# Where the later head pairs' position casts stand in an attention layer: other rounds, and the subtraction behind a round's last addition

## The chip, the cores and the metric

One core of a Trainium2 chip. The core has five engines, each with an instruction queue of its own: TensorE (PE, matrix products), VectorE (DVE), ScalarE (ACT), GpSimd (POOL) and SyncE (SP, which here only issues transfers). The metric is the device time of one execution of the whole program, in microseconds (us).

## The reference, cut to what matters

Eight images of 32 x 32 positions and 384 channels pass through a block with two layers. The part that the change touches is the attention of the first layer: six heads of width 64, with decomposed relative positions.

```python
# layer 0, x after a group norm; hw = 1024 positions, NH = 6, HD = 64
q, k, v = qkv[0], qkv[1], qkv[2]                      # (8 * 6, 1024, 64)
attn = jnp.einsum('bqd,bkd->bqk', q * SCALE, k)
rel_h = jnp.einsum('bhwc,hkc->bhwk', r_q, Rh)         # r_q is q as (b * NH, 32, 32, HD)
rel_w = jnp.einsum('bhwc,wkc->bhwk', r_q, Rw)
attn = attn.reshape(b * NH, h, w, h, w) + rel_h[:, :, :, :, None] + rel_w[:, :, :, None, :]
attn = jax.nn.softmax(attn.reshape(b * NH, hw, hw), axis=-1)
out = jnp.einsum('bqk,bkd->bqd', attn, v)
x = x + (out @ proj_w + proj_b)
```

Then follow a causal attention over the 1024 positions with one head of width 384, and, for five of the images, a feed-forward network (FFN) whose weights are binarized about group means and whose outputs are scaled by their largest absolute value.

## The kernel before, in words

**Images.** They are computed one after the other in the order 5, 0, 1, 2, 3, 4, 6, 7. Each runs through `layer0`, a projection, `attention1`, and, for images 0 to 4, the FFN.

**Pairs.** The six heads of layer 0 are handled as three pairs p = 0, 1, 2; the two heads of a pair lie on partitions 0 to 63 and 64 to 127. The text calls them pair 0, pair 1 and pair 2; pair 2 is the third.

**Position terms.** `positions(p)` (line 475) multiplies the queries with the tables of relative positions, and has the result written to memory and read back in another order (`near`). `place(p, near, pages)` (line 507) splits it in two parts[...]: for each of two halves d of the partitions ScalarE casts the values to the rounded type, `hi` (line 514, a 64 x 1024 copy), and VectorE subtracts, which leaves the remainder `lo` (line 515). Both lie in pages named `far`. Sixteen transfers then spread them over four pages `r`: the eight of `hi` are issued by SP, the eight of `lo` by GpSimd (line 522). For pair 0 this is done ahead of the attention. For pairs 1 and 2 `place` is a generator with two stops, called `later`, of which `attend0_fast` takes a piece of two steps (one pair) at a time.

**Rounds.** `attend0_fast` runs over (pair p, query half) in six rounds: (0, 0), (0, 1), (1, 0), (1, 1), (2, 0), (2, 1). The text calls them the first to the sixth. A round has these parts:

- `scores` (line 585), once for each of eight key tiles c of 128 positions: for the two heads two matmuls of queries and keys (line 590) into two tiles of PSUM, and two that add the position terms from `r` (line 594); then two exponentials on ScalarE (line 600) into a page `pr` of 128 x 1024.
- `add_up` (line 603): seven additions on VectorE (605 and 607) sum the eight pages to `sum0`, for the softmax's denominators. It returns the total and the sixth product's addition, `adds[4]`, the fifth of the seven.
- `reciprocals` (line 629) of the round before: two small matmuls into a PSUM tile `den` (line 633), behind this round's scores on PE; on VectorE, queued behind `adds[4]`, a reciprocal (637), `check` (two reductions to `seen`, lines 427 and 428; the one of line 427 reads `den` and is the tile's last reader), a broadcast copy to `wide` (641) and a transpose (642). GpSimd multiplies the output `oT` of the round before by it (line 659).
- `values` (line 610): 32 matmuls (line 615) of the exponentials with the values; ScalarE copies the result to `oT` (line 662).
- `over_tiles` (line 621): a transpose and a reduction on VectorE (624, 626), which make the operand `few` of the next `den`.

In the third round the image's input is loaded (`load_x`, SP) and GpSimd adds a bias to its eight pieces (`residual`, line 566, additions at 569), for use after the attention.

**PSUM.** All these matmuls write into tiles of one pool with eight banks, taken in turn; a tile's first write waits for the last reader of the tile that had the bank before. The score tiles of the fourth key tile come to the bank of the `den` tile of the round before.

**Order.** The lines are traced in this order, and a planner then fixes each engine's queue ahead of time by when it reckons an instruction's operands ready. `tc.issue_after(ins)` overrules it: what the block holds on `ins`'s engine is queued behind `ins` there. It sets an order of issue, not a wait for `ins` to finish, and does nothing to instructions on other engines. PE's order is written out by hand so (`behind_last`).[...]

For pair 1's pieces in the first round and pair 2's in the second, the kernel before asks this for ScalarE alone:

```python
if p == 0:
    with tc.issue_after(last_exp[0]):     # the round's last exponential, on ScalarE
        for _ in range(2):
            next(later, None)
```

So the casts stand behind all exponentials of the round, while the place of the subtractions on VectorE is left to the planner.

**Image 5**, the first, has work of its own in the same rounds: in its first, PE multiplies two weight matrices for the second layer (`multiply_out`); in its fifth (in the order of tracing) `binarize` is begun, which sums the FFN's weights group by group. The weights come by GpSimd in three loads (line 232), each a wide buffer, and each sum is a reduction on VectorE (line 250). The planner puts these where it reckons the loads landed, which may be rounds earlier than traced. Later pieces of `binarize` are taken between the key tiles of `attention1`.

A second, slower program for inputs outside the range stands behind a test at the end; it isn't executed with these inputs.

Of the kernel before, what the change touches and what calls it, by code (L numbers as in the profile page):

```python
# [11 lines left out]
F32 = mybir.dt.float32  # L12
# [3 lines left out]
ALU = mybir.AluOpType  # L16
# [9 lines left out]
NPAIR = NH // 2  # L26
# [49 lines left out]
def conv_attn_hybrid(  # L76
# [19 lines left out]
    nc = tc.nc  # L96
# [208 lines left out]
    def stages(pools):  # L305
# [120 lines left out]
        def check(total, reciprocal, i):  # L426
            nc.vector.tensor_reduce(seen[:, 0, i : i + 1], total, AX.X, ALU.add)  # L427
            nc.vector.tensor_reduce(seen[:, 1, i : i + 1], reciprocal, AX.X, ALU.add)
# [14 lines left out]
        def layer0(b, xT):  # L443
# [60 lines left out]
                            )  # L504
                return near, [page.bitcast(F32R) for page in pages]

            def place(p, near, pages):


                for d in range(2):  # L510
                    hi, lo, src = (t[ts(d, HD)].rearrange("k (h w) -> k h w", h=H) for t in (*pages, near))
                    if d:
                        src = near[ts(d, HD)].rearrange("k (w h) -> k h w", h=H)
                    nc.scalar.copy(hi, src)
                    nc.vector.tensor_tensor(lo, src, hi.bitcast(F32), ALU.subtract)  # L515
                    if d == 0:
                        yield
                for part in range(4):
                    for d in range(2):
                        for i in range(2):  # L520
                            half = part % 2 if d else part // 2
                            (nc.gpsimd if i else nc.sync).dma_start(  # L522
                                out=r[part][:, p, :].bitcast(F32).rearrange("(m i) t -> i m t", i=4)[2 * i + d],
                                in_=pages[i][ts(2 * d + 1 - half, 32)].bitcast(F32),
                            )
# [13 lines left out]
            near = []  # L539
# [9 lines left out]
            for j in range(NJ):  # L549
                values(j)  # L550
            r.extend(pools.image(f"r_{b}_{part}", F32R) for part in range(4))
            for _ in place(0, *near[0]):
                pass

            def others():
                for p in range(1, NPAIR):
                    yield from place(p, *near[p])
                    yield

            later = others()  # L560
            for _ in () if pools.fast else later:
                pass
            if pools.fast and b == ORDER[0]:
                join_biases(pools)

# [8 lines left out]
        def attend0_fast(residual, b, q, k, r, v, later):  # L574


            oT = pools.image(f"oT_{b}")

            rows = (slice(0, HD), slice(HD, P))
            last_exp, last_matmul = [None], [None]  # L580

            def behind_last():
                return tc.issue_after(last_matmul[0]) if last_matmul[0] is not None else contextlib.nullcontext()

            def scores(p, c, half):

                sc = [pools.o_tile(f"s0_{b}_{p}_{c}_{half}_{par}") for par in range(2)]
                with behind_last():
                    for par in range(2):
                        nc.tensor.matmul(  # L590
                            sc[par], k[rows[par], p, ts(c, P)], q[rows[par], p, ts(half, 512)], start=True, stop=False
                        )
                    for par in range(2):
                        last_matmul[0] = nc.tensor.matmul(  # L594
                            sc[par], unit[rows[par], c // 2 % 2].rearrange("i h w -> i (h w)"),
                            r[2 * (c // 4) + c % 2][rows[par], p, ts(half, 512)], start=False, stop=True,
                        ).ins
                pr = pools.page(f"pr0_{b}_{p}_{c}_{half}")
                for par in range(2):
                    last_exp[0] = nc.scalar.activation(pr[:, ts(par, 512)], sc[par], AF.Exp).ins  # L600
                return pr

            def add_up(p, half, prs):
                total = pools.page(f"sum0_{b}_{p}_{half}")
                adds = [nc.vector.tensor_tensor(total, prs[0], prs[1], ALU.add).ins]
                for pr in prs[2:]:
                    adds.append(nc.vector.tensor_tensor(total, total, pr, ALU.add).ins)  # L607
                return total, adds[4]

            def values(p, half, prs):  # L610
                av = pools.o_tile(f"av0_{b}_{p}_{half}")
                with behind_last():
                    for c, pr in enumerate(prs):
                        for par in range(2):
                            last_matmul[0] = nc.tensor.matmul(  # L615
                                av[ts(par, HD), :], v[:, c, ts(2 * p + par, HD)], pr[:, ts(par, 512)],
                                start=(c == 0), stop=(c == NJ - 1),
                            ).ins
                return av

            def over_tiles(p, half, total):

                tr = pools.page(f"tr0_{b}_{p}_{half}")
                nc.vector.transpose(tr, total)
                few = pools.small.tile([P, 2, 16], F32, tag="few", bufs=2, name=f"few_{b}_{p}_{half}")
                nc.vector.tensor_reduce(few, tr.rearrange("p (a n i) -> p a n i", a=2, i=32), AX.X, ALU.add)
                return few

            def reciprocals(p, half, few):
                den = pools.o_tile(f"den0_{b}_{p}_{half}")  # L630
                with behind_last():
                    for par in range(2):
                        last_matmul[0] = nc.tensor.matmul(
                            den[ts(par, HD), :16], fold.rearrange("p a i -> p (a i)"), few[:, par, :], start=True, stop=True
                        ).ins
                rt = pools.small.tile([P, 16], F32, tag="rt0", bufs=2, name=f"rt0_{b}_{p}_{half}")
                nc.vector.reciprocal(rt, den[:, :16])
                check(den[:, :16], rt, b * PER_IMAGE + 2 * p + half)
                room = pools.page(f"wide0_{b}_{p}_{half}")
                wide, rb = room[:, :512], room[:, 512:]  # L640
                nc.vector.tensor_copy(wide.rearrange("p (n i) -> p n i", i=32), rt.unsqueeze(2).to_broadcast([P, 16, 32]))
                nc.vector.transpose(rb, wide)
                return rb

            xt, waiting = None, None
            for p, half in itertools.product(range(NPAIR), range(2)):
                t, last = ts(half, 512), (p, half) == (NPAIR - 1, 1)
                prs = [scores(p, c, half) for c in range(NJ)]
                if b == ORDER[0] and (p, half) == (0, 0):
                    multiply_out(pools)  # L650
                if b == ORDER[0] and (p, half) == (2, 0):
                    signs.append(binarize(pools))
                    next(signs[0])
                total, late_add = add_up(p, half, prs)
                if waiting is not None:
                    p0, t0 = waiting[0], ts(waiting[1], 512)
                    with tc.issue_after(late_add):
                        rb = reciprocals(*waiting)
                    (nc.vector if last else nc.gpsimd).tensor_tensor(oT[:, p0, t0], oT[:, p0, t0], rb, ALU.mult)
                av = values(p, half, prs)  # L660
                if not last:
                    nc.scalar.copy(oT[:, p, t], av)
                if (p, half) == (1, 0):
                    xt = residual()
                if p == 0:
                    with tc.issue_after(last_exp[0]):
                        for _ in range(2):
                            next(later, None)
                waiting = (p, half, over_tiles(p, half, total))
            nc.vector.tensor_tensor(oT[:, p, t], av, reciprocals(*waiting), ALU.mult)  # L670
            with behind_last():
                begun = [project(wproj_sb, slice(0, C), oT, j, f"pj_{b}_{j}") for j in range(4)]

            def more(j):
                ps = begun[j] if j < 4 else project(wproj_sb, slice(0, C), oT, j, f"pj_{b}_{j}")
                nc.vector.tensor_tensor(xt[:, j, :], ps, xt[:, j, :], ALU.add)

            return xt, more
# [327 lines left out]
    with ExitStack() as scope:  # L1006
        pools = Pools(scope, tc, "f")
# [43 lines left out]
```

## Time and profile before

| | |
|---|---|
| Time, median of 3 runs | 2401.52 us (2399.17 to 2405.88) |
| The profiled execution | 2400.84 us |
| Its span, first to last instruction | 2399.1 us |
| Mean granted clock of TensorE | 0.992 |
| ScalarE busy | 1041.7 us (43%) |
| GpSimd busy | 329.9 us (14%) |
| Largest group of instructions on VectorE, the additions at line 607 | 377.4 us, 1311 ns each |
| Casts and subtractions for each image (lines 514 and 515) | six of each |

How to read it. The program is executed once with the hardware profiler on; all views come from this execution. The time is longer than the span by 1.7 us, which lie before the first and after the last instruction. Busy shares are means over stages with different limits. In the views an arrow `<-` inside a group's name stands for "made from", and an arrow after a duration names who released the waiting instruction; a number in square brackets at the end of a line is the idle time ahead of it. The two columns ahead of an instruction in a timeline are its start from the span's start and its duration, in us; `xN` says that N like it in a row are shown as one. In a table of stretches there follow the stretch's length and the busy time of PE, PE's weight loads, VectorE, ScalarE and GpSimd with the number of their instructions in brackets, the granted clock as a share of the full one, the mean busy share of the 16 transfer engines, and GB/s.

### The profile page before, as it was taken

Reading aid. Unit: us, or ns where it says so; the run is one execution under the profiler, and the core shown is the slowest. Engines: PE = TensorE matmul, PEld = TensorE weight load, DVE = VectorE, ACT = ScalarE, POOL = GpSimd, SP = SyncE. Lnnn points to the kernel's source line nnn. Section 1 sums busy time; section 2 is a strip of 40 time slices with the busy share of each in tenths; the row PEclk is TensorE's granted clock in tenths of the full one; section 3 lists DMA queues with packets and bytes.
Section 4 is the critical chain, followed back from the end, with each engine's and each line's share of the span. In section 5 each row is a group of like instructions: output and inputs, shape, how many; then the busy total and the mean of one; then the engine's idle time right before and its main releaser. Section 6 shows DMA issues by size and latency. Waiting matters only on the chain.

```text
span 2399.1 us, 26120 instructions
## 1 busy us (share of the span) xinstructions
PE 2347.1 (98%) x9442; PEld 1311.2 (55%) x9442; DVE 1441.9 (60%) x2302; ACT 1041.7 (43%) x1763; POOL 329.9 (14%) x421
## 2 busy tenths in 40 slices
PE   7899999999999999999999999999999999999998
PEld 3445544558644577445684455864457744554454
DVE  4585558655587347684455864558734668524851
ACT  3451155227463246551375522746424655115520
POOL 0310014000240001410002300024000131001300
PEclk9999999999999999999999999999999999999999
DMA  6610371220631012510108211053101271017100
GB/s 165 191 39 25 151 145 47 79 79 1 141 97 66 1 40 83 145 43 34 40 4 174 60 66 40 1 133 105 53 14 40 69 151 44 1 50 153 36 1 28
DMA packets 154795, 169.99 MB, mean 71 GB/s; under 512 B 113408, under 2 KB 126048, under 8 KB 153120
## 3 DMA queue, kind: packets, MB, share of 16 engines
q1 hardware_dynamic: 134416, 98.93, 16.4%
q0 software_dynamic: 17184, 69.22, 9.7%
q8 instruction: 77, 1.26, 0.2%
q10 hardware_dynamic: 3056, 0.08, 0.1%
q14 instruction: 62, 0.51, 0.1%
HBM read 75.38 MB, written 42.47 MB: 49 GB/s over the span
## 4 chain that ended last, share of the span: by engine, by line
PE 90%; DVE 5%; DMA 3%; SPq 1%; issue 1%; ACT 0%; POOL 0%; DVEq 0%; ACTq 0%
PE f_s L590 12%; PE f_av L615 11%; PE f_qk L438 10%; PE f_s L779 8%; PE f_av L792 8%; PE f_y L940 7%; PE f_y L899 7%; PE f_pj L386 5%; PE f_v L386 5%; PE f_q L738 5%; PE f_v L534 5%; PE f_s L594 4%; DVE f_sum L607 3%; PE f_rel L484 2%; DMA f_x<-in_x 1%; PE f_pt L314 1%
## 5 line engine op out<-in xcount | busy, mean ns | idle before, releaser
L600 ACT ACTIVATE f_pr<-f_s 128x512 f32<-128x512 f32 x768 | 413.5, 595 | 103.7 <-PE f_s L594 87.4
L590 PE MATMUL f_s<-f_q,f_k 64*128 64x512 f32 x1536 | 423.8, 611 | 27.3 <-DVE seen L427 27.3
L607 DVE TENSOR_TENSOR f_sum<-f_sum,f_pr 128x1024 f32<-128x1024 f32 x288 | 377.4, 1311 | 17.8 <-ACT f_pr L600 0.9
L615 PE MATMUL f_av<-f_pr,f_v 128*64 128x512 f32 x1536 | 339.3, 594 | 0.0
L594 PE MATMUL f_s<-f_r,unit 64*128 64x512 f32 x768 | 329.2, 808 | 0.2 <-DMA f_r<-f_far 0.2
L438 PE MATMUL f_qk<-f_gnT,wqkv_sb 128*128 128x512 f32 x576 | 257.3, 599 | 1.5 <-DVE f_gnT L349 1.5
L590 PEld LDWEIGHTS f_s<-f_q,f_k 64*128 64x128 f32 x1536 | 159.7, 191 | 157.5 <-issue 66.0
L615 PEld LDWEIGHTS f_av<-f_pr,f_v 128*64 128x64 f32 x1536 | 106.3, 137 | 196.4 <-issue 192.4
L779 PE MATMUL f_s<-f_q,f_lnT 128*128 128x512 f32 (+3 forms) x576 | 195.9, 488 | 0.0
L792 PE MATMUL f_av<-f_v,f_pr 128*128 128x385 f32 x576 | 195.3, 486 | 0.0
L438 PEld LDWEIGHTS f_qk<-f_gnT,wqkv_sb 128*128 128x128 f32 x576 | 108.0, 191 | 143.1 <-issue 131.1
L786 ACT ACTIVATE f_pr<-f_s 128x512 f32<-128x512 f32 (+3 forms) x96 | 47.1, 491 | 263.7 <-DVE f_s L784 217.6
L522 POOL DMA_DIRECT2D f_r<-f_far x192 | 102.6, 537 | 377.7 <-DVE f_far L515 343.9
L792 PEld LDWEIGHTS f_av<-f_v,f_pr 128*128 128x128 f32 x576 | 108.2, 190 | 77.3 <-issue 11.5
L779 PEld LDWEIGHTS f_s<-f_q,f_lnT 128*128 128x128 f32 x576 | 102.0, 190 | 77.8 <-issue 54.1
L594 PEld LDWEIGHTS f_s<-f_r,unit 64*128 64x128 f32 x768 | 86.6, 192 | 86.7 <-issue 83.1
L903 ACT ACTIVATE f_h<-f_y,b_sb 128x256 f32<-128x256 f32 x240 | 100.9, 471 | 67.3 <-PE f_y L899 67.3
L910 DVE TENSOR_REDUCE am<-f_h 128x1 f32<-128x1024 f32 (+2 forms) x80 | 71.6, 947 | 96.2 <-ACT f_h L903 96.2
L738 PE MATMUL f_q<-f_lnT,wqk 128*128 128x512 f32 x288 | 127.5, 592 | 0.0
L386 PE MATMUL f_pj<-wproj_sb,f_oT 128*128 128x384 f32 x384 | 127.3, 488 | 0.0
L386 PE MATMUL f_v<-wv_sb,f_lnT 128*128 128x384 f32 x384 | 126.5, 486 | 0.0
L534 PE MATMUL f_v<-wqkv_sb,f_gnT 128*128 128x384 f32 x384 | 125.1, 486 | 0.0
(153 smaller groups left out, 3036.0 us busy)
## 6 DMA issues: line engine op xcount, KB each, us to landing
f_far<-f_far SPq DMA_DIRECT2D x48, 512.0 KB, 3.2
f_r<-f_far POOLq DMA_DIRECT2D x192, 128.0 KB, 3.8
f_r<-f_far SPq DMA_DIRECT2D x192, 128.0 KB, 3.2
f_gnT<-in_xT SPq DMA_DIRECT2D x24, 512.0 KB, 4.6
f_x<-in_x SPq DMA_DIRECT2D x32, 384.0 KB, 6.4
out_y<-f_x POOLq DMA_DIRECT2D x28, 384.0 KB, 4.4
f_far<-f_far SPq DMA_DIRECT2D x128, 64.0 KB, 4.9
f_w1a<-w1s POOLq DMA_DIRECT2D x5, 1536.0 KB, 7.0
```

The source lines that it names most:

```text
L386: nc.tensor.matmul(ps[:, :C], xT[:, k, ts(j, P)], w[:, k, cols], start=(k == 0), stop=(k == NC - 1))
L438: nc.tensor.matmul(made[half], wqkv_sb[:, i, ts(m, P)], xT[:, i, ts(half, 512)], start=(i == 0), stop=(i == NC - 1))
L534: nc.tensor.matmul(ps, keys[:, i, j // 2, j % 2], wqkv_sb[:, i, 2 * C :], start=(i == 0), stop=(i == NC - 1))
L590: nc.tensor.matmul(sc[par], k[rows[par], p, ts(c, P)], q[rows[par], p, ts(half, 512)], start=True, stop=False)
L594: last_matmul[0] = nc.tensor.matmul(sc[par], unit[rows[par], c // 2 % 2].rearrange("i h w -> i (h w)"), r[2 * (c // 4) + c % 2][rows[par], ...
L600: last_exp[0] = nc.scalar.activation(pr[:, ts(par, 512)], sc[par], AF.Exp).ins
L607: adds.append(nc.vector.tensor_tensor(total, total, pr, ALU.add).ins)
L615: last_matmul[0] = nc.tensor.matmul(av[ts(par, HD), :], v[:, c, ts(2 * p + par, HD)], pr[:, ts(par, 512)], start=(c == 0), stop=(c == NJ - 1),
L738: nc.tensor.matmul(ps, wqk[:, k, ts(m, P)], xT[:, half, k, :], start=(k == 0), stop=(k == NC - 1))
L779: nc.tensor.matmul(sc[:, lo:], xT[:, c // 4, k, ts(c % 4, P)], q[:, half, k, lo:], start=(k == 0), stop=(k == NC - 1),)
L792: nc.tensor.matmul(av[:, : C + 1], prs[c][:, ts(j - c, P)], v[:, c, :], start=(c == 0), stop=(c == j))
L899: nc.tensor.matmul(ps, w1k[i // 2][:, ts(m, P)], xs[i % 2][:, half, i // 2, :], start=(i == 0), stop=(i == 2 * NC - 1))
```

## The change

`place` is an ordinary function now and takes two instructions, `behind`: the casts are queued behind the first of them on ScalarE, the subtractions behind the second on VectorE. `add_up` hands back all seven additions. `attend0_fast` calls for pair 1's casts in the first round, as before, and for pair 2's in the third instead of the second; in both the casts stand behind the round's last exponential, as before, and the subtractions behind the round's last addition. `reciprocals` stands behind the sixth product's addition, as before.

```diff
-            def place(p, near, pages):
-
+            def place(p, near, pages, behind=(None, None)):
+
+                def after(ins):
+                    return contextlib.nullcontext() if ins is None else tc.issue_after(ins)
 
                 for d in range(2):
...
-                    nc.scalar.copy(hi, src)
-                    nc.vector.tensor_tensor(lo, src, hi.bitcast(F32), ALU.subtract)
-                    if d == 0:
-                        yield
+                    with after(behind[0]):
+                        nc.scalar.copy(hi, src)
+                    with after(behind[1]):
+                        nc.vector.tensor_tensor(lo, src, hi.bitcast(F32), ALU.subtract)
...
-            for _ in place(0, *near[0]):
-                pass
-
-            def others():
-                for p in range(1, NPAIR):
-                    yield from place(p, *near[p])
-                    yield
-
-            later = others()
-            for _ in () if pools.fast else later:
-                pass
+            place(0, *near[0])
+
+            def later(p, *behind):
+                place(p, *near[p], behind)
+
+            for p in () if pools.fast else range(1, NPAIR):
+                later(p, None, None)
...
-                return total, adds[4]
+                return total, adds
...
-                total, late_add = add_up(p, half, prs)
+                total, adds = add_up(p, half, prs)
                 if waiting is not None:
                     p0, t0 = waiting[0], ts(waiting[1], 512)
-                    with tc.issue_after(late_add):
+                    with tc.issue_after(adds[4]):
                         rb = reciprocals(*waiting)
...
-                if p == 0:
-                    with tc.issue_after(last_exp[0]):
-                        for _ in range(2):
-                            next(later, None)
+                if half == 0 and p + 1 < NPAIR:
+                    later(p + 1, last_exp[0], adds[-1])
                 waiting = (p, half, over_tiles(p, half, total))
```

## The prediction

> **What bounds the kernel now.** I read four views, in this order: the page's busy times, the waits of PE, the timeline of one image around the longest of these waits, and a table of stretches over the same microseconds.
>
> The page, first and second block:
>
> ```profile
> span 2399.1 us, 26120 instructions
> PE 2347.1 (98%) x9442; PEld 1311.2 (55%) x9442; DVE 1441.9 (60%) x2302; ACT 1041.7 (43%) x1763; POOL 329.9 (14%) x421
> ```
>
> PE is busy for 98%, so only what PE does not do (52 us of idle), or does slowly, can be won. The waits of PE, in the view of waits limited to PE:
>
> ```profile
> PE f_s L590 <- DVE seen L427: 27.3, 8, 8.2
> PE f_gmean L336 <- DVE gmv L333: 10.8, 1, 10.8
> PE f_bad L201 <- DVE worst L199: 1.9, 1, 1.9
> ```
>
> More than half of the idle time is one wait, eight times: once per image. The score matmuls of the third round (pair 1, half 0) wait for `check`'s reduction `seen`, the last reader of a PSUM tile `f_den`, because the fourth key tile's scores take that tile's bank. Timeline of image 0 (image 5 is computed first, then 0, 1, 2, 3, 4, 6, 7), VectorE's instructions and then PE's:
>
> ```profile
> 356.98 1.22 DVE L605 TENSOR_TENSOR f_sum<-f_pr,f_pr 128x1024 f32<-128x1024 f32 x1
> 358.30 1.23 DVE L607 TENSOR_TENSOR f_sum<-f_sum,f_pr 128x1024 f32<-128x1024 f32 x1
> 361.19 1.22 DVE L515 TENSOR_TENSOR f_far<-f_far 64x1024 fp32r<-64x1024 f32 x1 [1.67 <-ACT f_far L514]
> 362.34 2.02 DVE L607 TENSOR_TENSOR f_sum<-f_sum,f_pr 128x1024 f32<-128x1024 f32 x1
> 364.39 2.56 DVE L515 TENSOR_TENSOR f_far<-f_far 64x1024 fp32r<-64x1024 f32 x1
> 366.98 3.82 DVE L607 TENSOR_TENSOR f_sum<-f_sum,f_pr 128x1024 f32<-128x1024 f32 x2
> 370.72 0.24 DVE L637 RECIPROCAL rt<-f_den 128x16 f32<-128x16 f32 x1
> 372.65 0.16 DVE L427 TENSOR_REDUCE seen<-f_den 128x1 f32<-128x16 f32 x1
> ...
> 369.36 1.02 PE L590 MATMUL f_s<-f_q,f_k 64*128 64x512 f32 x2
> 372.87 1.22 PE L590 MATMUL f_s<-f_q,f_k 64*128 64x512 f32 x1 [2.49 <-DVE seen L427]
> ```
>
> Pair 2's subtractions (L515) stand between the additions of the second round. They need ScalarE's casts (L514), which stand behind the round's last exponential, so VectorE idles 1.67 us with ready additions behind it; the reciprocal stands behind the sixth product's addition and comes 12 us after its matmul.
>
> The stretches (second round, third, fourth; the gap; what follows it):
>
> ```profile
> 349.93:365.99 16.06, 16.06 (x86) 6.84 (x85) 14.08 (x11) 12.29 (x19) 8.73 (x10) 1.00 0.81 226
> 365.99:388.63 22.64, 20.15 (x86) 10.68 (x85) 21.79 (x21) 9.25 (x17) 16.25 (x15) 0.85 0.28 75
> 388.63:404.69 16.06, 16.06 (x86) 6.90 (x84) 15.62 (x20) 9.23 (x17) 1.70 (x2) 1.00 0.00 0
> 370.38:372.87 2.49, 0.00 (x1) 0.00 (x0) 2.49 (x5) 0.33 (x1) 2.49 (x2) 0.85 0.00 0
> 372.87:378.20 5.33, 5.33 (x16) 4.20 (x18) 5.33 (x6) 2.09 (x4) 5.32 (x8) 0.50 0.20 44
> ```
>
> A round takes 16.06 us, the third 22.64. Of the 6.58 us over, 2.49 are idle; the rest is that PE then runs at half clock (0.50) for 5.33 us. From the timeline, the third round's excess over 16.06 is, in order of execution: 11.89, 6.58, 5.59, 3.66, 6.99, 5.34, 5.86, 3.87 us. Sum 49.8; without image 5, 37.9.
>
> **The Trainium skill.** "TensorE: Matmul & The Clock Gate", section "What's actually happening": an idle PE falls to half clock and needs about 3.4 us of work to come back. The trace agrees (0.50), though here a gap of 2.49 us is enough. "Perfetto Trace Analysis", section "Tensor Engine Instruction (MATMUL, LD_WEIGHTS)": VectorE's and ScalarE's queues are strictly first in, first out; the 1.67 us show it. "SBUF — State Buffer", section "Who interferes with whom": a VectorE instruction with two SBUF inputs and a GpSimd one that reads SBUF exclude each other. Agrees: beside GpSimd's L569 additions an addition takes 1.84 to 2.02 us, else 1.23, and L569 takes 1.94 us, else 0.97.
>
> **The change part by part.** It adds and removes no work: 32 casts, 32 subtractions and the same transfers. As built, PE's and SP's orders are unchanged; ScalarE's casts of pair 2 stand behind the third round's exponentials instead of the second's. VectorE's and GpSimd's orders move.
>
> *First round.* Additions no longer wait for the casts. In image 0 they start at 337.58 as now, one each 1.33 us, and the last ends at 346.8; casts end at 345.7 and 347.2; two subtractions 1.22 and 1.91, transpose 1.25, reduction 1.22 end at 352.2 (now 357.06). The den matmuls are at 358.86: covered by 6.7 us. Pair 1's GpSimd transfers leave with the subtractions, within 1 us of now (346.71, 349.79); they are needed at 366.
>
> *Second round.* No subtraction. Two exponential pairs are done at 353.5; five additions at 1.33 end at 360.1; reciprocal 0.25, an addition now beside L569 (1.9), `seen` 0.16: done at 362.5. PE needs it at 370.4. Cover 7.9 us, so the wait and the half clock behind it go. For the seven later images: **-37.9 us**. What is late next: nothing within the round, since PE then runs as in the fourth to sixth (9.06 us of scores, 7.0 of values).
>
> *Third round, which gets pair 2's work.* Starts 365.99. Exponentials allow additions from 369.6; L569 runs to 375.5, so three at 1.91 and two at 1.33: fifth done at 378.0. Reciprocal, addition, `seen` at 379.8, needed at 382.05+4.4=386.4: cover 6.6. Last addition 381, copy 0.42, then subtraction (casts done at 379.3), wide transpose 0.67, subtraction, transpose 1.25, reduction 1.22. The subtractions cost 1.22 to 2.6 each; I take 1.2 and 1.9 (the first pair in the trace): end 387.8, at worst 389.8. The den matmuls are at 391.0: cover 3.2, or 1.2. The fourth round's additions then start at 387.8 instead of 385.9; its `seen` comes at 395.9 and is needed at 402.5. By the fifth round VectorE is back in step.
>
> *Transfers of pair 2.* SP's eight follow the casts (376.1, 379.2) and are issued by 386. GpSimd's eight (0.53 each) stand behind the two `oT` multiplications (1.3 to 2.3) and end near 390, landing median 3.8: 394. The fifth round needs the first page at 398.7. Cover 5. SP's input loads stand ahead of them as now, and the next image's load stands behind them, at the sixth round. So the move itself costs nothing.
>
> *Image 5* has more on VectorE: the sums over the FFN weights (L250). As built, these now stand between the second round's additions, and GpSimd issues the first weight load behind all eight L569 additions instead of four. Eight at 0.97, two of them slowed, from 96 to 105; landing took 6.6 (99.98 to 106.61): 111.6. Three sums at 0.72 and three additions at 1.22 put the reciprocal at 117.4 and `seen` at 119.0, now 120.98: this stall shrinks by 2. Then the second weight load, into the same buffer, must wait for all five sums: issued near 125, its two parts landed at 130.6 and 133.2 (medians 5.1 and 7.0). Ten sums at 0.39 stand in front of the third round's additions: these start at 135.2, now 128.73. `seen` comes at 143.2 (6.45 to the reciprocal, 1.5 more), while PE, starting the fourth round at 134.4, needs it at 138.8. A new stall of 4.4, and half clock: in the seven images a mean wait of 2.7 costs 5.4, so 2.7 more. **+7.1 - 2.0 = +5.1 us**; bounds -2 (no new stall) and +12 (loads 5 us later).
>
> Sum: -37.9 + 5.1 = -32.8. The profiled execution took 2400.84 us (span 2399.1), the median of the runs is 2401.52. 2400.84 - 32.8 = 2368.0, or 2368.7 on the median's footing: **2369 us**.
>
> **Rivals.**
> 1. *Image 5 is freed too.* Loads land sooner than VectorE reaches them; -40 to -50: 2352 to 2361. For it: its wait is on a transfer, not on arithmetic. Against: two loads in one buffer, with sums in front of additions.
> 2. *The wait is partly handed on.* The third round's reduction comes after 391, so PE waits at den and runs cold in the fourth round. Cover is only 1.2 to 3.2 us. A miss of 0.5 us costs about that; with some half clock 2 per image, 16 in all: 2376 to 2390.
> 3. *Slower.* Pair 2's pages come too late for the fifth round: GpSimd's queue holds them behind `oT`, which waits for the wide transpose, and a subtraction waits for the cast. Against: 5 us of cover. It decides when they slip by 7.5 us: 2.5 of stall and 2.7 of half clock in eight images are 42 us against 32.8 won; 2410.
> 4. *It doesn't do what it says.* The bank is held by something else once the additions are early: 2400. Against: as built, PE's fourth key tile waits for just this `seen` in every round, and rounds four to six run without stall.
>
> **How the numbers follow.** Forecast (seven images freed, image 5 with one or two stalls, 2361 to 2375) 0.68; rival 1 0.10; rival 2 0.12; rival 3 0.06; rival 4 0.04. A measurement of this kernel tells some 0.3%, 7 us, from no change. Faster: 0.68 + 0.10 + most of rival 2 = 0.89; same 0.05; slower 0.06. The range takes the forecast with half of rivals 1 and 2: 2359 to 2381.
>
> **What would show it.** Right: in the seven images the third round takes 16.1 us, the wait of L590's scores for `seen` is left in image 5 alone, some 10 us in two pieces, and the clock is 1.00 in every other third round. The reduction of the third round ends before den's matmuls. Wrong: a wait of den for `few` or of the r matmuls for a transfer, a fourth round over 16.1 us in images after the first, or VectorE still idle in front of subtractions with additions behind.

## The result and the profile after

| | before | changed |
|---|---|---|
| Time, median | 2401.81 us (4 runs, 2399.17 to 2405.88) | 2371.46 us (4 runs, 2370.05 to 2372.34) |
| Ratio to before, 95% interval | | 0.9873 [0.9858, 0.9888] |
| The profiled execution, and its span | 2400.84 us, 2399.1 us | 2370.05 us, 2367.9 us |
| Excess of the third round over 16.06 us, seven images, sum | 37.9 us | 0.0 us |
| Image 5: excess of its third and fourth round | 11.9 and 0.0 us | 10.6 and 7.35 us |

The change is 1.3% faster. The page after, its first lines (span; busy time, share of the span and instructions of each engine):

```profile
span 2367.9 us, 26177 instructions
PE 2332.1 (98%) x9442; PEld 1291.8 (55%) x9442; DVE 1431.8 (60%) x2302; ACT 1042.0 (44%) x1763; POOL 312.2 (13%) x421
```

PE is still busy for 98%, of a span that is 31 us shorter. The view of PE's waits (total, times, longest):

```profile
PE f_s L588 <- DVE seen L427: 11.9, 2, 7.4
PE f_gmean L336 <- DVE gmv L333: 10.8, 1, 10.8
```

The wait for `seen` is left twice instead of eight times, and both are in image 5. (Lines behind the diff are two lower than before, so the scores are L588 and L592; inside it the subtractions are now L519 and the transfers of the pages L524.) The table of stretches for image 0, second, third and fourth round, answers to the one shown of before:

```profile
357.74:373.80 16.06, 16.06 (x86) 6.84 (x84) 14.44 (x15) 9.18 (x17) 8.64 (x11) 1.00 0.71 207
373.80:389.87 16.07, 16.07 (x87) 6.91 (x85) 13.43 (x15) 12.31 (x19) 6.51 (x8) 1.00 0.12 29
389.87:405.93 16.06, 16.06 (x87) 6.93 (x85) 15.53 (x18) 9.22 (x17) 6.99 (x9) 1.00 0.38 103
```

The third round took 22.64 us and takes 16.07; PE's clock is 1.00 in it. VectorE's timeline in the same image shows why:

```profile
362.72 5.21 DVE L605 TENSOR_TENSOR f_sum<-f_sum,f_pr 128x1024 f32<-128x1024 f32 x4
367.85 0.25 DVE L635 RECIPROCAL rt<-f_den 128x16 f32<-128x16 f32 x1
368.04 1.23 DVE L605 TENSOR_TENSOR f_sum<-f_sum,f_pr 128x1024 f32<-128x1024 f32 x1
369.18 0.17 DVE L427 TENSOR_REDUCE seen<-f_den 128x1 f32<-128x16 f32 x1
...
388.28 1.21 DVE L519 TENSOR_TENSOR f_far<-f_far 64x1024 fp32r<-64x1024 f32 x1
389.42 0.69 DVE L640 STREAM_TRANSPOSE f_wide<-f_wide 128x512 f32<-128x512 f32 x1
390.14 1.97 DVE L519 TENSOR_TENSOR f_far<-f_far 64x1024 fp32r<-64x1024 f32 x1
392.14 1.25 DVE L622 STREAM_TRANSPOSE f_tr<-f_sum 128x1024 f32<-128x1024 f32 x1
393.42 1.22 DVE L624 TENSOR_REDUCE few<-f_tr 128x32 f32<-128x1024 f32 x1
```

The read of `den` now ends at 369.35, 4.45 us before the third round begins (before: 6.82 us after its beginning). Pair 2's subtractions, at 388.28 and 390.14, cost 3.2 us of VectorE, and the reduction still ends at 394.64 with the `den` matmuls at 398.79.

The span is shorter by 31.2 us: 37.9 won in the seven images, 6.0 lost in image 5, and 0.7 lost elsewhere: 1.56 us before image 5's first round (it starts at 72.03 instead of 70.47, in work that the change doesn't touch), of which 0.9 come back in small pieces.

Image 5's two stalls, from VectorE's timeline of the changed kernel:

```profile
98.94 1.84 DVE L605 TENSOR_TENSOR f_sum<-f_sum,f_pr 128x1024 f32<-128x1024 f32 x1
114.71 0.79 DVE L250 TENSOR_REDUCE sums_w<-f_w 128x1 f32<-128x614 f32 x1 [13.92 <-DMA f_w<-in_w1T]
115.42 1.22 DVE L605 TENSOR_TENSOR f_sum<-f_sum,f_pr 128x1024 f32<-128x1024 f32 x1
...
121.55 0.17 DVE L427 TENSOR_REDUCE seen<-f_den 128x1 f32<-128x16 f32 x1
...
126.14 1.48 DVE L250 TENSOR_REDUCE sums_w<-f_w 128x1 f32<-128x614 f32 x2
132.62 4.09 DVE L250 TENSOR_REDUCE sums_w<-f_w 128x1 f32<-128x307 f32 x10 [5.00 <-DMA f_w<-in_w1T]
136.62 1.22 DVE L603 TENSOR_TENSOR f_sum<-f_pr,f_pr 128x1024 f32<-128x1024 f32 x1
```

Each time a weight sum that waits for its load (13.92 us, then 5.00) stands ahead of additions whose operands are ready.

### The profile page after: what moved, and what is told of

Same layout as the page of the kernel before. It is cut to its first block, busy times and chain, and to the rows that moved or that the text cites. A ratio compares the mean times of both kernels' runs of the same rounds, so it can differ in the third digit from the quotient of the medians.

```text
span 2367.9 us, 26177 instructions
## 1 busy us (share of the span) xinstructions
PE 2332.1 (98%) x9442; PEld 1291.8 (55%) x9442; DVE 1431.8 (60%) x2302; ACT 1042.0 (44%) x1763; POOL 312.2 (13%) x421
## 3 DMA queue, kind: packets, MB, share of 16 engines
q8 instruction: 77, 1.26, 0.2%
## 4 chain that ended last, share of the span: by engine, by line
PE 95%; DVE 2%; DMA 1%; POOL 0%; issue 0%; ACT 0%; SPq 0%; DVEq 0%; POOLq 0%; ACTq 0%
PE f_s L588 13%; PE f_av L613 13%; PE f_qk L438 11%; PE f_s L775 8%; PE f_av L788 8%; PE f_y L936 7%; PE f_y L895 7%; PE f_pj L386 5%; PE f_v L386 5%; PE f_v L536 5%; PE f_q L734 5%; PE f_s L592 3%; PE f_rel L484 2%; PE f_pt L314 1%; DVE f_sum L605 1%; PE f_den L631 0%
## 5 line engine op out<-in xcount | busy, mean ns | idle before, releaser
L588 PE MATMUL f_s<-f_q,f_k 64*128 64x512 f32 x1536 | 404.7, 600 | 11.9 <-DVE seen L427 11.9
L605 DVE TENSOR_TENSOR f_sum<-f_sum,f_pr 128x1024 f32<-128x1024 f32 x288 | 364.4, 1265 | 22.4 <-DVE rt L635 0.6
L592 PE MATMUL f_s<-f_r,unit 64*128 64x512 f32 x768 | 311.5, 797 | 0.0
L588 PEld LDWEIGHTS f_s<-f_q,f_k 64*128 64x128 f32 x1536 | 148.1, 188 | 140.7 <-issue 74.1
L524 POOL DMA_DIRECT2D f_r<-f_far x192 | 102.5, 536 | 462.3 <-DVE f_far L519 418.9
L592 PEld LDWEIGHTS f_s<-f_r,unit 64*128 64x128 f32 x768 | 76.9, 188 | 91.2 <-issue 90.7
```

The lines of the kernel that those rows point to most:

```text
L588: nc.tensor.matmul(sc[par], k[rows[par], p, ts(c, P)], q[rows[par], p, ts(half, 512)], start=True, stop=False)
L592: last_matmul[0] = nc.tensor.matmul(sc[par], unit[rows[par], c // 2 % 2].rearrange("i h w -> i (h w)"), r[2 * (c // 4) + c % 2][rows[par], ...
```

## The experiments

All times below are medians, beside runs of the kernel before on the same chip. "Seven" is the sum of the excess over 16.06 us in the second to fifth rounds of the seven images other than 5.

| kernel | median us | ratio to before, 95% | seven, us | image 5's excess, us |
|---|---|---|---|---|
| second_gated | 2365.56 | 0.9845 [0.9829, 0.9862] | 0.0 | 12.9 and 0.8 |
| third_free | 2362.10 | 0.9835 [0.9819, 0.9852] | 0.8 | 9.1 and 0.1 |
| first_free | 2362.15 | 0.9832 [0.9816, 0.9849] | 0.0 | 9.4 and 0.0 |
| sums_late | 2354.39 | 0.9797 [0.9781, 0.9813] | 0.0 | 0.0 |
| sums_spread | 2354.36 | 0.9801 [0.9787, 0.9815] | 0.0 | 0.0 |
| read_late_3 | 2377.58 | 0.9897 [0.9880, 0.9913] | 4.2 | 20.2 |
| read_late_5 | 2404.98 | 1.0012 [1.0004, 1.0021] | 30.1 | 23.1 |
| read_late_7 | 2434.46 | 1.0135 [1.0118, 1.0152] | 51.8 | 26.4 |
| before_read_early | 2425.48 | 1.0101 [1.0084, 1.0118] | 43.6 | 10.4 |
| fourth_round | 2419.01 | 1.0069 [1.0053, 1.0085] | 41.9 | 10.2, 7.6 and 7.3 |

First rounds aren't counted: image 5's carries other work, in every kernel alike, and one of another image is now and then 1 us longer for a transfer. The time of a kernel isn't the sum of its row: other stages differ by 1 to 2 us between kernels, and `before_read_early` loses 2.15 us more in each image's last round.

### Which part of the change brings it

Pair 2's casts back in the second round, with the order on VectorE kept:

```diff
-                if half == 0 and p + 1 < NPAIR:
-                    later(p + 1, last_exp[0], adds[-1])
+                if p == 0:
+                    later(half + 1, last_exp[0], adds[-1])
```

> The changed kernel, but pair 2's casts go back to the second round; its subtractions stand behind that round's last addition. Theory A (only the place of the subtractions on VectorE matters: the additions and the read of the den tile must not stand behind them): the third round of images 0 to 4, 6, 7 takes 16.06 us as with the change, the reduction of the second round ends near 31 us after the round before began and PE's den doesn't wait. Rival B (the second round has no room for this work, the move is what helps): the den matmuls of the third round wait for the reduction, or the third round takes 1 to 4 us over 16.06 in the seven images, 7 to 28 us in all. Image 5: the sum over the second weight load stands between the third round's fourth and fifth addition instead of ten sums before the first one, so its second stall (7.35 us over) falls to 0 to 2 and the first stays near 10.6. In all A: 2363 to 2367 us; B: 2371 to 2395.

Measured: 2365.56 us, no excess in the seven images; the second round's reduction ends 1.9 to 3.9 us before `den` needs it. Rival B falls: the second round has the room. The move isn't needed if the order is there. Image 5's first stall is 12.9 us, where I had expected it to stay near 10.6.

The move alone, subtractions left to the planner:

```diff
-                    later(p + 1, last_exp[0], adds[-1])
+                    later(p + 1, last_exp[0], None)
```

> The changed kernel without the order on VectorE: pair 2's casts in the third round, subtractions placed by the planner, which puts pair 2's behind the second and the third addition of the third round. Theory A, worked out from the changed kernel's trace of image 0: casts end at 385.5 and 387.0, so subtractions and additions run until the reciprocal at 392.5, the read of den ends at 394.0, and PE needs it at 394.3: the fourth round takes 16.1 to 17.5 us in the seven images, so that the move alone brings nearly everything, 2365 to 2385. Rival C (the order is what helps, the move only carries the stall one round on): the fourth round is 4 to 7 us over in each, as the third was before, 2395 to 2405. Image 5: its five first sums now stand ahead of the second round's additions and one of the second load's between them, first stall 13 to 18 us, second 0 to 3.

Measured: 2362.10 us, below the range that I gave; the fourth round takes 16.16 to 16.20 us in the seven images. Rival C falls too. VectorE's timeline of image 0 in this kernel (its third round began at 363.92):

```profile
371.76 2.12 DVE L605 TENSOR_TENSOR f_sum<-f_sum,f_pr 128x1024 f32<-128x1024 f32 x1
375.14 1.22 DVE L519 TENSOR_TENSOR f_far<-f_far 64x1024 fp32r<-64x1024 f32 x1 [1.26 <-ACT f_far L517]
376.28 1.21 DVE L605 TENSOR_TENSOR f_sum<-f_sum,f_pr 128x1024 f32<-128x1024 f32 x1
377.52 1.95 DVE L519 TENSOR_TENSOR f_far<-f_far 64x1024 fp32r<-64x1024 f32 x1
379.50 2.48 DVE L605 TENSOR_TENSOR f_sum<-f_sum,f_pr 128x1024 f32<-128x1024 f32 x2
381.91 0.25 DVE L635 RECIPROCAL rt<-f_den 128x16 f32<-128x16 f32 x1
382.07 1.17 DVE L605 TENSOR_TENSOR f_sum<-f_sum,f_pr 128x1024 f32<-128x1024 f32 x1
383.17 0.17 DVE L427 TENSOR_REDUCE seen<-f_den 128x1 f32<-128x16 f32 x1
```

The subtractions stand between additions, and VectorE idles 1.26 us for a cast, as in the kernel before. But GpSimd's bias additions, beside which VectorE's took longer in the kernel before, are over at 370.40, before the first of these lines, and the read ends 3.35 us into the fourth round, 0.1 late. So each half of the change frees the seven images by itself. The move alone does it with nothing to spare; the order alone (`second_gated`) has 6.3 to 7.7 us of cover for the read and 1.9 for the reduction.

The order taken off in the first round only:

```diff
-                    later(p + 1, last_exp[0], adds[-1])
+                    later(p + 1, last_exp[0], adds[-1] if p else None)
```

> The changed kernel, but pair 1's subtractions in the first round aren't held behind the last addition; pair 2's are, in the third. Theory A: in the seven images nothing changes (no round over 16.1 us), since the first round's reduction has 6.7 us of cover; that part of the change is worth nothing there. In image 5 the planner then puts five sums ahead of the second round's additions and one of the second load's between them: first stall 13 to 18 instead of 10.6, second 0 to 3 instead of 7.35; 2367 to 2376. Rival: the first round's part carries some of the gain, the second or the third round of the seven images is 2 to 6 us over again, 2385 to 2400.

Measured: 2362.15 us, below what I expected and 9.3 us faster than the change. In the seven images nothing moves, as expected. In image 5 the planner now puts GpSimd's first weight load between its bias additions again (issued at 101.12 us, not 107.34), which shortens the first stall and takes the second away; my 13 to 18 us for the first stall assumed the late load. So the first round's part of the change brings nothing and, through the planner, costs 8.5 us in image 5 (17.9 of excess against 9.4), more than the 6.0 that image 5 lost. The expectation for image 5 was wrong for `third_free` in the same way.

### Image 5

The weight sums behind the last multiplication of the attention (`sums_behind[0]`):

```diff
-            nc.vector.tensor_tensor(oT[:, p, t], av, reciprocals(*waiting), ALU.mult)
+            sums_behind[:] = [nc.vector.tensor_tensor(oT[:, p, t], av, reciprocals(*waiting), ALU.mult).ins]
...
-                    next(work, None)
+                    with tc.issue_after(sums_behind[0]):
+                        next(work, None)
...
```

> The changed kernel with the FFN weights' sums of image 5 held on VectorE behind the last multiplication of its attention. Theory A (the two stalls of image 5 are its weight sums standing ahead of additions): image 5's third and fourth round take 16.1 us like the others', 17.9 us won there; the sums (3.6 us and 4.1 us of VectorE) then stand among the projection's additions, which costs 0 to 4 us; 2352 to 2358. Rival (image 5's stalls come from elsewhere, from the transfers of pair 2 or the multiplication of the weight matrices): the third or the fourth round stays 4 us or more over; 2362 to 2372.

Measured: 2354.39 us, 17.1 us less than the change; all of image 5's rounds from the second on take 16.05 to 16.12 us. PE's waits of this kernel, the longest first:

```profile
PE f_gmean L336 <- DVE gmv L333: 11.4, 1, 11.4
PE f_bad L201 <- DVE worst L199: 1.9, 1, 1.9
PE f_qk L438 <- DVE f_gnT L349: 1.5, 1, 1.5
PE f_pt L314 <- DVE f_xn L376: 1.5, 2, 1.2
```

The wait for `seen` is gone. The price is in the last line: 1.5 us of waiting for the layer norm behind the attention, where the sums now stand. So I spread them, begun in the fourth round, two pieces behind each round's last addition and the rest as above:

```diff
-                if g % 2:
+                if g in (2, 4):
                     yield False
...
-                if b == ORDER[0] and (p, half) == (2, 0):
+                if b == ORDER[0] and (p, half) == (1, 1):
...
+                if b == ORDER[0] and signs:
+                    with tc.issue_after(adds[-1]):
+                        for _ in range(2):
+                            next(signs[0])
...
```

> The changed kernel with image 5's weight sums spread: binarize is begun in the fourth round, the first load's five sums stand behind the fourth round's last addition, the second load's ten behind the fifth's and the sixth's, the last five behind the last multiplication. Theory A: each place has room (VectorE reads den 6 to 7 us ahead of need in these rounds), so all six rounds of image 5 stay as in the other images, and the 1.5 us that the layer norm waited in the kernel with all sums at the end go too: 2352 to 2355 us, at most 1.5 below that kernel. Rival: a sum waits for its load in front of VectorE's other work, and the fifth or sixth round of image 5 is 1 us or more over: 2355 to 2365.

Measured: 2354.36 us, no different. The layer norm's wait fell to 0.3 us, and a wait of `den` for the reduction, 1.87 us, came behind the last round: five sums stand in front of that reduction. So not every place had the room that I had assumed.

### What PE waits for, and what lateness costs

In the second round, reciprocal and read stand behind the round's reduction and behind 3, 5 or 7 added reductions that compute nothing of use:

```diff
...
+                few, behind = None, adds[4]
+                if (p, half) == (0, 1):
+                    few = over_tiles(p, half, total)
+                    behind = last_few[0]
+                    for _ in range(5):
+                        with tc.issue_after(behind):
+                            behind = nc.vector.tensor_reduce(spare, wqkv_sb[:, 0, :T], AX.X, ALU.add).ins
...
-                    with tc.issue_after(adds[4]):
+                    with tc.issue_after(behind):
...
```

> The changed kernel, but in the second round the reciprocal and the read of den are queued on VectorE behind the round's transpose and reduction and behind three added reductions of 128x1024 (1.22 us each) over a weight tile, whose results nobody uses. Theory A (PE needs that read by 4.4 us into the third round and by nothing earlier): counted from image 0 of the changed kernel's trace, the last addition ends near 371, the reduction at 373.4, the read near 377.4, PE needs it at 378.2: the third round of the seven images stays at 16.1 us, although VectorE reads den 8 us later than with the change. Rival D (the cover isn't what I worked out, something else of the read's chain is needed earlier): the third or fourth round takes 1 us or more over 16.06. Image 5 may move by up to 8 us either way. A: 2363 to 2380 us in all, D: 2380 to 2400.

> The same with five added reductions. Theory A: the read ends near 379.9 where PE needs it at 378.2, a gap of some 1.7 us in each of the seven images. If such a gap costs its own length alone: third rounds of 17.8 us, 12 us in all; if PE falls to half clock behind it as behind the gaps of 2.5 to 3.1 us before the change, 1.1 to 4.1 us more in each: 18.9 to 21.9 us. Rival D's price (the read isn't what PE waits for): no change against three.

> The same with seven. Theory A: a gap of 4.1 us in each of the seven images, half clock behind it for sure, 1.1 to 4.1 us more: third rounds of 21.3 to 24.3 us, the stall of before the change and more, with the subtractions behind the additions all the same; 2405 to 2432 us. Rival D: no change against three.

With five and seven reductions the stall came back at its old place, with the subtractions behind the additions all the while. What was delayed is the whole of `reciprocals` on VectorE, not its read alone; but PE's view names only `seen` for these rounds, and the round's reduction, now ahead of it, ends 9.5 us or more before the matmuls of `den`. Rival D's forecast for five and seven, no change, failed. Its sign for three, a round 1 us or more over, did come: four images are 0.6 to 1.4 us over, two of them more than 1, because the read is needed at 3.2 us and not at the 4.4 that I had worked out. `read_late_7` lies 2.5 us above its range; much of what these three lose is in image 5 (20 to 26 us), where the delayed read stands behind weight sums as well. The three kernels, with those above, give a curve. "Read" is the end of the read (L427, here L428) after the start of the round that needs the bank, "excess" that round's time over 16.06 us:

| read, us | excess, us | where |
|---|---|---|
| 3.21 to 3.22 | 0.0 | read_late_3, three images |
| 3.33 to 3.37 | 0.10 to 0.14 | third_free, seven |
| 3.83, 4.19, 4.45, 4.61 | 0.60, 0.97, 1.23, 1.39 | read_late_3, the other four |
| 5.71 to 5.72 | 2.5 | read_late_5, two |
| 6.34 to 6.39 | 4.7 to 4.85 | read_late_5, four |
| 6.88 and 7.09 | 3.7 and 3.9 | before, two |
| 6.82 to 7.42 | 5.3 to 7.0 | before, the other five |
| 7.56 | 6.0 | read_late_5, one |
| 8.23 to 8.92 | 6.4 to 8.0 | read_late_7, seven |

Up to 2.5 us of lateness against 3.23 us the excess is that lateness, to 0.03 us. Beyond, half clock comes on top: in the seven images 0 to 3.0 us, near 1.67 in half of the cases (the last section has the reason). PE's clock (last column but two) behind the gap in image 0 of `read_late_5`:

```profile
384.30:387.00 2.70, 2.70 (x8) 1.51 (x10) 2.56 (x5) 0.17 (x1) 1.36 (x1) 0.50 0.00 0
387.00:390.00 3.00, 3.00 (x18) 1.39 (x14) 2.90 (x2) 2.29 (x5) 0.73 (x1) 0.92 0.02 5
```

The other way round: the kernel before, where only the read comes earlier, behind the fourth product's addition:

```diff
-                return total, adds[4]
+                return total, adds[2]
```

> The kernel before with one number changed: the reciprocal and the read of den stand behind the fourth product's addition instead of the sixth's, in every round; casts and subtractions stay in the first and second round, one of pair 2's subtractions still between the second round's additions. Theory A (the bank's release is all that PE waits for): in image 0's trace of before the first subtraction ends at 362.4, one addition, the read near 366, PE needs it at 370.4: the third round falls from 19.7 to 23 us to 16.1 in the seven images, 37.9 us won without moving a cast. Image 5 gets five weight sums ahead of the second round's additions and one of the second load's ahead of its reduction: its excess is 6 to 16 us against 11.9. In all 2358 to 2370. Rival E (the subtractions among the additions, or the time at which pair 2's pages are ready, hold PE in another way as well): third or fourth round 1 us or more over in the seven images, 2372 to 2400.

Measured: 2425.48 us, 23.8 slower than before; my expectation failed, and rival E's range of 2372 to 2400 was too low as well. Its longest wait of PE (total, times, longest):

```profile
PE f_den L633 <- DVE few L626: 48.3, 16, 4.5
```

And a piece of VectorE's timeline of image 0:

```profile
366.95 0.16 DVE L427 TENSOR_REDUCE seen<-f_den 128x1 f32<-128x16 f32 x1
...
374.04 2.57 DVE L515 TENSOR_TENSOR f_far<-f_far 64x1024 fp32r<-64x1024 f32 x1
376.64 1.25 DVE L624 STREAM_TRANSPOSE f_tr<-f_sum 128x1024 f32<-128x1024 f32 x1
377.92 1.22 DVE L626 TENSOR_REDUCE few<-f_tr 128x32 f32<-128x1024 f32 x1
```

The read ends at 367.11, 0.5 us into the third round that began at 366.61, and the wait for `seen` is gone in the seven images, so the bank was what PE waited for. But the round's reduction ends at 379.1, and `den` is due at 375.5: a second limit, as late as the first, had stood behind it. The kernel before has it too (its reductions end 3.1 to 3.8 us after the `den` matmuls would be due in an unstalled round), and no wait shows it there, because PE was already late. What stood between the additions made everything behind them late, read and reduction; in the changed kernel the second round's reductions end 6.7 to 8.1 us before `den` needs them.

### How late pair 2's pages may come

The casts one round later still, in the fourth:

```diff
-                if half == 0 and p + 1 < NPAIR:
+                if (p, half) in ((0, 0), (1, 1)):
                     later(p + 1, last_exp[0], adds[-1])
```

> The changed kernel, but pair 2's casts one round later still, in the fourth; order on VectorE as in the change. Tests the slower case of the prediction (pair 2's pages too late for the fifth round) and the 5 us of cover that the change leaves it. From image 0 of the changed kernel: the second GpSimd transfer, with which the first page is whole, is issued by 393.7 and lands 3.9 later, 397.6, the last near 400.8; the fifth round needs the first page at 406.5. A round later these are 413.6 and 416.9: PE's position matmuls of the fifth round wait 7 to 10 us for a transfer in each of the eight images, and half clock adds 0 to 3: fifth rounds of 23 to 29 us, 56 to 106 in all, 2427 to 2477 us. Rival (the pages aren't what bounds the place, VectorE is): the loss is in the reads of den or in the reductions, and the fifth round stays at 16.1.

Measured: 2419.01 us. The fifth round of the seven images takes 21.5 to 23.2 us, 49.2 us over in all with image 5's; I had expected 23 to 29 and at least 2427. In GpSimd's timeline of image 0 (fifth round from 412.93) the second transfer, the first of the last line, completes the first page:

```profile
411.51 0.72 POOL L524 DMA_DIRECT2D f_r<-f_far  x1 [12.75 <-DVE f_far L519]
412.26 2.62 POOL L657 TENSOR_TENSOR f_oT<-f_oT,f_wide 128x512 f32<-128x512 f32 x1
414.83 3.72 POOL L524 DMA_DIRECT2D f_r<-f_far  x7
```

It is issued at 414.8 to 415.4, and the first position matmul, due 0.57 us into the round, runs at 417.50. PE's view of waits names no releaser there (30.5 us stand under "issue"), so that PE waited for this transfer is worked out from the order of the transfers. If so, it landed within some 2.1 us, where I had taken the median of 3.9, and its issue came 1.4 us earlier in its round than in the changed kernel, where bias additions run beside VectorE's. The direction is shown: the fifth round's position matmuls are what is late (the reads that it needs end 4.7 us or more before it begins), so the pages bound how far the casts may move. One round is free and two are not.

## Why the prediction was right

2369 us were predicted, 2371.46 measured; for the profiled execution 2368.0 and 2370.05.

- **The seven images, -37.9 us: right** to the tenth; their third rounds take 16.05 to 16.08 us.
- **The cover of the read.** Predicted 7.9 us, from a read 3.5 us ahead of the third round and a need 4.4 us into it. Measured 7.7: the read 4.45 ahead, and the need 3.23 into it. Two terms were off by 1 us and cancelled, which is luck. The need was taken from where PE's gap begins in the record, and the curve shows that this is 1.2 us too late.
- **What the prediction left out.** It gave the second round's cover for the read alone. `before_read_early` shows that the second round's reduction stood behind it, 3.1 to 3.8 us late for `den`. The change brings both in time, so the 37.9 us came whole; the sum had a reason for one of the two only, and in this it was lucky.
- **The first round.** Cover of its reduction 6.7 us predicted, 6.4 measured. That gating wasn't needed there: without it 1.8 us are left, as before the change.
- **The third round.** Cover of the reduction predicted 3.2, measured 4.15 in image 0; the read that the fourth round needs ends 3.2 us ahead of it, predicted 2.2. Nothing was handed on (rival 2).
- **The transfers** (rival 3). No position matmul waits in the changed kernel. `fourth_round` shows that the risk was real and where it begins.
- **Rival 4**, another holder of the bank, is excluded by `read_late_5`, `read_late_7` and `before_read_early`.
- **Image 5, +5.1 us: measured +6.0.** The first stall shrank by 1.3 us, not 2.0: the load landed at 114.7 instead of the 111.6 worked out. The second stall was 7.35 us, predicted 7.1. That the weight sums, where they stood, make both is shown by `sums_late`. What the prediction didn't see is that the order in the first round, not needed for its own purpose, is what sent the load behind the bias additions.
- **Idle and half clock.** The prediction read 2.49 us idle and the rest of 6.58 as half clock in image 0. But 5.33 us at half clock can cost 2.7 us at most, not 4.1. By the curve 3.6 are waiting and 3.0 half clock. The sum, which is what the forecast used, is the same.

## What to carry to other kernels

When an instruction that waits for another engine is put among ready ones in a queue that keeps its order, as VectorE's did here, ask what stands behind it and for whom: 1.7 us of idle VectorE and a few slowed additions became 4 to 7 us an image on PE. A stall that a profile names may hide a second one of the same size, so repair the queue that makes both late rather than the instruction that was named; moving the named read alone made this kernel slower. And look at the places where the same edit has no use: an order that costs nothing where it stands can still change what a planner does with other work.

## What the runs showed that I had not expected

The record of waits understates the loss. In four images of `read_late_3` the third round is 0.6 to 1.4 us longer and PE's waits list none; over the eight rounds of the kernel before, the view names 27.3 us where the lateness against 3.23 us sums to 36.2. The reason is in PE's timeline, here image 3 of `read_late_3`, from the third key tile on (the round began at 1322.91, the read ended at 1327.52):

```profile
1325.20 1.02 PE L589 MATMUL f_s<-f_q,f_k 64*128 64x512 f32 x4
1325.66 0.80 PE L593 MATMUL f_s<-f_r,unit 64*128 64x512 f32 x2
1326.30 1.02 PE L589 MATMUL f_s<-f_q,f_k 64*128 64x512 f32 x2
1326.75 0.80 PE L593 MATMUL f_s<-f_r,unit 64*128 64x512 f32 x1
1327.58 1.13 PE L589 MATMUL f_s<-f_q,f_k 64*128 64x512 f32 x4
```

Four records of a key tile take 1.02 us, and so do two: the two heads' matmuls run side by side, each head on its half of the rows (their records start in pairs, 0.01 us apart). At the fourth key tile one head's go on, from 3.4 to 4.6 us into the round, while the other's wait for the bank. The time is lost, and PE counts as busy.

Half clock isn't a matter of the gap's length alone. PE lost nothing beyond the wait at 2.5 us of lateness, about 1.6 to 1.7 at 3.1, and again nothing in two images of the kernel before at 3.65 and 3.86. "TensorE: Matmul & The Clock Gate", section "What's actually happening" of the Trainium skill, speaks of a free-running window of about 3.4 us, and of half clock after a window of idling. The clock records agree with the first and not with the second. In each trace half clock begins and ends, but for the program's end, on one grid of steps of 3.413 us; in the kernel before, image 0's begins at 372.14 and image 1's at 696.40, 95 steps later. Image 0, and then image 2, step by step (the second line is two steps):

```profile
368.73:372.14 3.41, 1.65 (x8) 0.55 (x4) 3.38 (x4) 1.92 (x4) 3.41 (x3) 1.00 0.05 17
372.14:378.97 6.83, 6.10 (x19) 4.82 (x19) 6.83 (x9) 2.17 (x4) 6.79 (x10) 0.50 0.25 64
1010.35:1013.76 3.41, 2.77 (x14) 1.14 (x10) 3.38 (x4) 3.02 (x6) 3.41 (x3) 1.00 0.31 85
1013.76:1017.17 3.41, 1.51 (x9) 1.31 (x11) 3.41 (x3) 0.34 (x1) 3.41 (x4) 1.00 0.00 0
1017.17:1020.59 3.42, 3.42 (x22) 2.75 (x18) 3.42 (x6) 3.33 (x7) 3.19 (x6) 1.00 0.71 194
```

Image 2's recorded gap, 2.54 us, is the longer one, but it falls on two steps and PE keeps its clock. What counts is PE's recorded idle time within a step. Over the twelve traces (25 to 2340 us), a step at full clock with 1.9 us of it or more was followed by half clock in 40 of 40 cases, one with 0.3 to 1.5 us in none of 46; in between it went both ways (5 of 14). At half clock, a step with up to 0.55 us of idle time was followed by full clock (45 of 45), one with 0.62 or more by half clock again (39 of 39). So about half a step of idle time was enough, where the page asks for a whole window, and the prediction's remark on the gap of 2.49 us stands.

With that the curve closes: in every late round of the kernel before and the three `read_late` kernels the excess is the lateness against 3.23 us and half of the half-clock time behind the read, to 0.1 us. A whole step costs 1.7 us; the 3.0 and 2.2 us are two steps that began before the read had ended.
